# Two attention scores moved beside the attention outputs, and steps moved in the first and last groups of a two-layer graph kernel

## The chip, the cores and the metric

The kernel runs on one core of a Trainium2 chip, as one program for both layers. The metric is the device time of one execution in microseconds. Steps are called by the names that the code's own lists give them, and engines by TensorE (PE, with its weight loads PEld), VectorE (DVE), ScalarE (ACT), GpSimd (POOL) and SyncE (SP, which only issues DMAs here).

## The reference, cut to what matters

The input x is 128 graphs of 128 nodes with 512 features, adj a 128x128 matrix that all share. Everything is float32.

```python
# layer 0
h = relu(layernorm(x))
q, k, v = h @ Wq.T, h @ Wk.T, h @ Wv.T
rel = adj.T * (q @ k.T)
rel = rel / norm(rel, axis=2)
x = x + rel @ v
# layer 1: 8 heads of 64
h = relu(layernorm(x))
q, k, v = h @ Wq + bq, h @ Wk + bk, h @ Wv + bv
weights = softmax(q @ k.T / sqrt(64) + where(adj == 0, -1e9, 0))
x = x + weights @ v
```

## The kernel before, in words

**Groups and products.** Four graphs make a group (G = 4), so there are 32 groups, and a product of weights with a group's h has 512 columns. Layer 0 folds Wq and Wk into one matrix "a", so it has two products per group, G (with "a", giving gT) and V. Layer 1 has three: Q, K and V. Each product is done by a Strassen-like scheme of seven products of 256x256 quarters: class Product has steps P1 to P7, each of four matmuls of 128x128 weights and 256 columns, which show in the profile as eight MATMUL instructions of line L218. The seven use sums of weight quarters (`sums`, L88, done once) and sums of h's quarters (sumA and sumB, four additions on VectorE in each group and layer). P1, P5 and P6 are copied out of PSUM (`keep`, for layer 0, Q and K on ScalarE, for layer 1's V on VectorE), P2, P3 and P7 are added to what was kept (L242, VectorE), P4 is copied. P1, P6, P7 and P4 pile up in the same PSUM bank "x", so P4's matmuls wait for P7's addition and P6's for P1's copy; P5 and P3 share bank "z", P2 has bank "y". The pool ps_mm has four banks for all products.

**The rest of a group.** Layer 0: R (L382) is h.T with gT, mask_rel and square follow on VectorE and ScalarE, N (L408) sums the squares in four tiles of 128x32, norms turns them, O (L422) is rel times v, xO adds to x. Layer 1: S (L453) is the score of one graph for eight heads, in two row tiles of 64x128; mk adds the mask and takes the maximum (VectorE), ex takes exponentials (ScalarE, eight instructions with their sums) and sends e to DRAM, wr fetches it with its blocks turned, wt turns within blocks (VectorE). A (L570) is the output of two graphs, in two column tiles of 128x64; oc copies and sends, rdo fetches, ot turns, scales and adds to x (VectorE, then GpSimd with the store). h is turned in the same way: stat and inv (statistics, VectorE and GpSimd), hn (ScalarE, sends), rd (SP, fetches), T (VectorE). A number behind a step is its graph or pair of graphs; S0 to S3 are the four scores of a group, A0 and A1 its two outputs.

**Buffers that tie steps together.** The tiles that rd, wr and rdo fetch into (u, pool tpool) have two buffers. gT of layer 0 and v1 of layer 1 share one buffer (tag pgv). A score fills its PSUM buffer alone (ps_s has one), so S waits for the ex before it. hn, e and oT share three buffers.

**The order of work.** All five engines run in a written order: `run` (L644) walks a list of steps, and each step's instructions are queued on their engines in that order. In a cycle, l is the group in layer 1, m the next group in layer 0, n is m's layer 1 that is being prepared, f the group after it whose x is being loaded, p is l's predecessor whose outputs are being finished. FIRST (L611) is the cycle of group 0, SECOND (L618) of group 1, ORDER (L627) of groups 2 to 31, that is 30 times, LAST (L637) finishes group 31. Ahead of FIRST stand the statistics of groups 0 and 1, the DMA issues of load and load1, the folding of "a" (weights0, L117, matmuls of line L123, evicted by `place` and followed by `sums`) and the turning of layer 0's Wv (weights_v0, L133, transposes of line L139). Weights1 has layer 1's weight sums. The part of each list that TensorE does:

```python
# ORDER, TensorE's steps before the change
Q1 Q2 K1 K2 Q5 Q6 Q3 A1 Q7 K5 K6 Q4 K3 K7 G1 K4 G2 S0 G5 G6 G3 V1 G7 V2 G4 S1 V5
R V6 V3 N S2 V7 O0 O1 V4 l.V1 O2 O3 S3 l.V2 l.V5 l.V6 l.V3 l.V7 A0 l.V4
```

The last group takes S2 and S3 in halves (mkA, exA, mkB, exB), turns e on TensorE (tw), takes An for A and ends with fin, whose addition to x is on GpSimd but for the last graph, and whose store SP issues.

Of the kernel before, what the change touches and what calls it, by code (L numbers as in the profile page):

```python
# [11 lines left out]
ALU = mybir.AluOpType  # L12
# [3 lines left out]
G = 4  # L16
# [5 lines left out]
def kernel(  # L22
# [15 lines left out]
    nc = tc.nc  # L38
# [29 lines left out]
    def load(g: int, b: int, queue):  # L68
        xb = xpool.tile([P, D], F32, tag="xb", name=f"xb_{g}_{b}")
        queue.dma_start(xb, x[g * G + b])  # L70
        x_tiles[g, b] = xb
# [16 lines left out]
    def sums(n: str, w12, eng):  # L88
        c = wc[n]
        eng.tensor_tensor(c[:, T1], w12, c[:, W11], ALU.subtract)  # L90
        eng.tensor_tensor(c[:, T2], c[:, W22], c[:, T1], ALU.subtract)
        eng.tensor_tensor(c[:, T3], c[:, W22], w12, ALU.subtract)
        eng.tensor_tensor(c[:, T4N], c[:, W21], c[:, T2], ALU.subtract)
# [16 lines left out]
    w12 = {}  # L110

    def place(n: str, m: int, ps, w12, copy):

        copy(wc[n][:, W11 if m < 2 else W21, m % 2, :], ps[:, 0:HF])
        copy(w12[:, m, :] if m < 2 else wc[n][:, W22, m % 2, :], ps[:, HF:D])

    def weights0(between):  # L117

        a12 = rpool.tile([P, 2, HF], F32, tag="r", name="a12")
        pa = [ps_mm.tile([P, D], F32, tag="mm", name=f"pa_{m}") for m in range(KD)]  # L120
        for k in range(KD):
            for m in range(KD):
                nc.tensor.matmul(  # L123
                    pa[m], lhsT=raw["q"][:, k, ts(m, P)], rhs=raw["k"][:, k, :],
                    start=(k == 0), stop=(k == KD - 1),
                )
            if k == KD - 2:
                between()
        for m in range(KD):
            place("a", m, pa[m], a12, nc.vector.tensor_copy)  # L130
        sums("a", a12, nc.vector)

    def weights_v0():  # L133

        v12 = rpool.tile([P, 2, HF], F32, tag="r", name="v12")
        for m in range(KD):
            pt = ps_mm.tile([P, KD, P], F32, tag="mm", name=f"pwv_{m}")
            for k in range(KD):
                nc.tensor.transpose(pt[:, k, :], raw["v"][:, k, ts(m, P)], ident)  # L139
            place("v0", m, pt.rearrange("p k e -> p (k e)"), v12, nc.scalar.copy)  # L140
        sums("v0", v12, nc.gpsimd)
        nc.vector.tensor_scalar(mask, adj_sb, 0.0, NEG, ALU.is_equal, ALU.mult)

    def load1():
        for name, w in (("q", wq1), ("k", wk1), ("v1", wv1)):
            wr = w.rearrange("(k p) d -> p k d", p=P)
            nc.gpsimd.dma_start(
                wc[name][:, W11 : W21 + 1].rearrange("p h k d -> p (h k) d"), wr[:, :, 0:HF]
            )
            nc.gpsimd.dma_start(wc[name][:, W22], wr[:, 2:4, HF:D])  # L150
            w12[name] = wpool.tile([P, 2, HF], F32, tag="wT", name=f"w12_{name}")
            nc.gpsimd.dma_start(w12[name], wr[:, 0:2, HF:D])
        nc.gpsimd.dma_start(bq_sb, bq1.rearrange("(e p) -> p e", p=P))
        nc.gpsimd.dma_start(bk_sb, bk1.rearrange("(e p) -> p e", p=P))
        nc.gpsimd.dma_start(bv_sb, bv1.partition_broadcast(P))

    class Weights1:
        def scale(self):

            SC = HD**-0.5  # L160
            nc.scalar.mul(wc["q"][:, 0:3], wc["q"][:, 0:3], SC)
            nc.scalar.mul(w12["q"], w12["q"], SC)
            nc.scalar.mul(bq_sb, bq_sb, SC)

        def sumq(self):
            sums("q", w12["q"], nc.vector)
# [199 lines left out]
    class Layer0(Layer):  # L366
        n = 0
# [62 lines left out]
    class Layer1(Layer):  # L430
        n = 1
# [104 lines left out]
        def fin(self, b):  # L536
            g, xb = self.g, x_tiles.pop((self.g, b))
            o = work.tile([P, D], F32, tag="o", name=f"o_{g}_{b}")
            nc.vector.tensor_tensor(
                o.rearrange("p (k r d) -> p k r d", k=NH, r=2),  # L540
                self.po.pop(b).rearrange("p (k r d) -> p k r d", k=NH, r=2),
                self.rs.pop(b).rearrange("p (r k) -> p k r", r=2)[:, :, :, None].to_broadcast(
                    [P, NH, 2, HD]
                ),
                ALU.mult,
            )
            (nc.vector if b == G - 1 else nc.gpsimd).tensor_tensor(xb, xb, o, ALU.add)
            nc.sync.dma_start(out[g * G + b], xb)

        def mkA(self, b):  # L550
# [58 lines left out]


    FIRST = """  # L611
        m.sumA m.sumB m.start m.G.P1 f.hn0 f.rd0 m.G.P2 m.G.P5 w.scale m.G.P6 w.sumq m.G.P3 m.V.P1 f.hn1 f.rd1
        w.sumv m.G.P7 m.V.P2 w.sumk m.G.P4 m.V.P5
        m.R m.mask_rel m.square f.T0 m.V.P6 m.V.P3 m.N m.norms m.V.P7 m.O0 m.xO0 m.O1 m.xO1 n.stat0 n.stat1
        n.inv0 m.V.P4 n.hn0 n.rd0 f.T1 m.O2 m.O3 f.sumA f.start f.G.P1 m.xO2 m.xO3 n.stat2 n.stat3 n.inv1
        f.G.P2 f.sumB f.G.P5 n.hn1 n.rd1 f.G.P6 f.G.P3 f.G.P7 n.T0 f.G.P4 n.T1 n.start
    """.split()
    SECOND = """  # L618
        l.Q.P1 l.sumA l.Q.P2 l.sumB l.K.P1 l.K.P2 l.Q.P5 l.Q.P6 f.load0 f.load1 l.Q.P3 l.K.P5 l.K.P6 l.Q.P7
# [1 line left out]
        m.V.P2 l.S1 l.mk1 m.V.P5  # L621
        l.ex1 l.wr1 l.wt0 m.R m.mask_rel m.square f.stat2 f.stat3 f.inv1 m.V.P6 m.V.P3 m.N m.norms l.S2 l.mk2
        m.V.P7 l.ex2 l.wr2 l.wt1 m.O0 m.xO0 m.O1 m.xO1 n.stat0 n.stat1 n.inv0 m.V.P4 n.hn0 n.rd0 l.start_v l.V.P1
        m.O2 m.xO2 m.O3 m.xO3 n.stat2 n.stat3 n.inv1 l.S3 l.mk3 l.V.P2 l.V.P5 n.hn1 l.V.P6 l.wt2 n.rd1 l.ex3
        l.wr3 l.V.P3 l.V.P7 n.T0 l.A0 l.oc0 l.V.P4 n.T1 n.start
    """.split()
    ORDER = """  # L627
        l.Q.P1 p.rdo0 l.sumA l.Q.P2 m.hn0 l.sumB l.K.P1 m.rd0 m.hn1 l.K.P2 m.rd1 p.wt3 l.Q.P5
        p.ot0 l.Q.P6 l.Q.P3 p.A1 p.oc1 p.rdo1 m.T0 l.Q.P7 l.K.P5 m.T1 l.K.P6 l.Q.P4 f.load0 f.load1
        l.K.P3 m.sumA l.K.P7 m.sumB m.start m.G.P1 l.K.P4 m.G.P2 l.S0 l.mk0 m.G.P5 m.G.P6 l.ex0 l.wr0  # L630
        p.ot1 m.G.P3 m.V.P1 m.G.P7 f.stat0 f.stat1 f.inv0 m.V.P2 f.load2 f.load3 m.G.P4 l.S1 l.mk1 m.V.P5
        l.ex1 l.wr1 l.wt0 m.R m.mask_rel m.square f.stat2 f.stat3 f.inv1 m.V.P6 m.V.P3 m.N m.norms l.S2 l.mk2
        m.V.P7 l.ex2 l.wr2 l.wt1 m.O0 m.xO0 m.O1 m.xO1 n.stat0 n.stat1 n.inv0 m.V.P4 n.hn0 n.rd0 l.start_v l.V.P1
        m.O2 m.xO2 m.O3 m.xO3 n.stat2 n.stat3 n.inv1 l.S3 l.mk3 l.V.P2 l.V.P5 n.hn1 l.V.P6 l.wt2 n.rd1 l.ex3
        l.wr3 l.V.P3 l.V.P7 n.T0 l.A0 l.oc0 l.V.P4 n.T1 n.start
    """.split()
    LAST = """  # L637
        l.Q.P1 p.rdo0 l.sumA l.Q.P2 l.sumB l.K.P1 l.K.P2 p.wt3 l.Q.P5 p.ot0 l.Q.P6 l.Q.P3 l.K.P5 l.K.P6 l.K.P3
        l.Q.P7 l.S0 l.mk0 l.K.P7 l.Q.P4 l.ex0 l.wr0 l.K.P4 l.S1 l.mk1 p.A1 p.oc1 p.rdo1 l.start_v l.V.P1
        l.ex1 l.V.P2 l.V.P5 l.S2 l.mkA2 l.mkB2 l.V.P6 l.exA2 l.exB2 l.wt0 l.wr1 l.V.P3 l.V.P7 l.S3 l.mkA3 l.mkB3  # L640
        l.tw2 l.wt1 l.exA3 l.exB3 l.V.P4 l.An0 l.fin0 l.An1 l.fin1 p.ot1 l.tw3 l.An2 l.fin2 l.An3 l.fin3
    """.split()
# [1 line left out]
    def run(order, **who):  # L644
        for step in order:
            name, *path = step.split(".")
            at = who.get(name)
            if at is None:
                continue
            if len(path) == 2:  # L650
                getattr(getattr(at, path[0]), path[1])()
            elif path[0][-1].isdigit():
                getattr(at, path[0][:-1])(int(path[0][-1]))
            else:
                getattr(at, path[0])()

    with tc.manual_schedule(engines={EN.PE, EN.SP, EN.Pool, EN.DVE, EN.Activation}):
        p, l, m = None, None, Layer0(0)
        for b in range(G):
            m.stat(b)  # L660
        m.inv(0)
        m.inv(1)
        for b in range(G):
            load(1, b, nc.gpsimd)
        load1()
        m.hn_pe(0)
        m.hn_pe(1)
        f = Layer0(1)
        for b in range(G):
            f.stat(b)  # L670
        f.inv(0)
        f.inv(1)
        weights0(lambda: m.turn_pe(0))
        m.turn_pe(1)
        weights_v0()
        for g in range(NG):
            n = Layer1(g)
            if g:
                f = Layer0(g + 1) if g + 1 < NG else None
            run((FIRST, SECOND, ORDER)[min(g, 2)], p=p, l=l, m=m, n=n, f=f, w=Weights1())  # L680
            p, l, m = l, n, f
        run(LAST, p=p, l=l)
# [30 lines left out]
```

## Time and profile before

| what | us |
|---|---|
| median of three runs | 2524.23 (2522.88 to 2525.54) |
| the profiled execution | 2526.15 |
| its span, first to last instruction | 2524.4 |
| TensorE busy (matmuls) | 2497.9 |
| VectorE, ScalarE, GpSimd busy | 1709.2, 1022.3, 534.7 |
| a steady cycle (from one l.Q.P1 to the next) | 77.14 |
| first matmul, last matmul's end | 4.29, 2514.8 |

TensorE's matmuls overlap: one is listed with the time from its start to its end, while the next starts before that end. So durations of matmuls are read from start to start. The mean granted clock of TensorE is 0.997 of full speed.

### The profile page before, as it was taken

The numbers are of one execution on the slowest core, as the hardware profiler recorded it, in microseconds if no ns is written. First come the engines' busy times: TensorE is split into PE (matmuls) and PEld (weight loads), VectorE is DVE, ScalarE is ACT, GpSimd is POOL, SyncE is SP. The second block draws the span as 40 slices with busy tenths as digits, with TensorE's granted clock in tenths as the row PEclk, the third lists the DMA queues.
The fourth block names the chain that finished last, engine by engine and source line by source line (L and its number), as shares of the span: only waits on it lengthen the run. The fifth ranks groups of instructions, "written<-read, shape, count | busy, mean of one in ns | idle before, by whom it ended". The sixth has DMA issues, their size and how long they took to land.

```text
span 2524.4 us, 40790 instructions
## 1 busy us (share of the span) xinstructions
PE 2497.9 (99%) x14672; PEld 2106.7 (83%) x14672; DVE 1709.2 (68%) x2484; ACT 1022.3 (40%) x3248; POOL 534.7 (21%) x945
## 2 busy tenths in 40 slices
PE   8999999999999999999999999999999999999998
PEld 6788888888888888888888888888888888888886
DVE  5566766676776667666767766676667676666766
ACT  3344443444433444344444434443444444344433
POOL 4121222112122212221121222122211212221211
PEclk9999999999999999999999999999999999999999
DMA  5255554556445555445564455554455644555543
GB/s 172 84 176 175 166 156 141 182 161 199 147 145 159 176 175 167 152 147 176 160 197 146 144 165 173 178 167 152 147 175 162 197 148 143 164 176 176 167 135 101
DMA packets 370475, 405.71 MB, mean 161 GB/s; under 512 B 29600, under 2 KB 286752, under 8 KB 370272
## 3 DMA queue, kind: packets, MB, share of 16 engines
q1 hardware_dynamic: 278992, 167.92, 25.2%
q10 hardware_dynamic: 70384, 166.74, 18.4%
q0 software_dynamic: 20896, 68.44, 8.2%
q8 instruction: 115, 1.88, 0.3%
q14 instruction: 88, 0.72, 0.1%
HBM read 204.80 MB, written 198.18 MB: 160 GB/s over the span
## 4 chain that ended last, share of the span: by engine, by line
PE 97%; DVE 1%; DMA 1%; ACT 0%; issue 0%; POOL 0%; SPq 0%; ACTq 0%; DVEq 0%; POOLq 0%
PE pv_x L218 18%; PE pq_x L218 9%; PE pv_z L218 9%; PE pk_x L218 9%; PE pg_x L218 9%; PE pss L453 6%; PE po L570 5%; PE pv_y L218 5%; PE pg_z L218 4%; PE pq_z L218 4%; PE pr L382 4%; PE pk_z L218 4%; PE po L422 4%; PE pk_y L218 2%; PE pg_y L218 2%; PE pq_y L218 2%
## 5 line engine op out<-in xcount | busy, mean ns | idle before, releaser
L471 ACT ACTIVATE e<-pss,nmax 128x128 f32<-128x128 f32 x1008 | 354.1, 379 | 178.0 <-DVE nmax L464 156.2
L605 POOL TENSOR_TENSOR xb<-xb,o 128x512 f32<-128x512 f32 x124 | 158.3, 1276 | 1108.8 <-DVE o L598 1083.9
L218 PE MATMUL pv_x<-wc_v,h 128*128 128x256 f32 x1280 | 300.8, 382 | 0.0
L218 PEld LDWEIGHTS pv_x<-wc_v,h 128*128 128x128 f32 x1280 | 240.3, 190 | 51.0 <-DVE v L242 11.8
L301 ACT ACTIVATE hn<-xb,shift,rstd 128x512 f32<-128x512 f32 x252 | 190.9, 807 | 153.5 <-POOL shift L293 153.4
L313 DVE STREAM_TRANSPOSE h<-u_h 128x1024 f32<-128x1024 f32 x126 | 156.4, 1242 | 133.0 <-DMA u_h<-d_h 130.4
L218 PE MATMUL pv_z<-wc_v,s 128*128 128x256 f32 x1024 | 246.0, 383 | 0.0
L471 ACT ACTIVATION_READ_ACCUMULATOR e<-pss,nmax 128x1 f32 x1008 | 220.7, 219 | 0.0
L218 PEld LDWEIGHTS pv_z<-wc_v,s 128*128 128x128 f32 x1024 | 192.6, 191 | 29.2 <-DVE pv_r L235 0.4
L462 DVE TENSOR_TENSOR pss<-pss,mask 128x1024 f32<-128x1024 f32 x126 | 154.7, 1228 | 81.0 <-PE pss L453 75.5
L218 PE MATMUL pv_x<-wc_v,s 128*128 128x256 f32 x768 | 184.9, 384 | 0.0
L218 PE MATMUL pq_x<-h,wc_q 128*128 128x256 f32 x768 | 184.8, 383 | 0.0
L283 DVE BATCH_NORM_STATS2 st<-xb 128x6 f32<-128x512 f32 x256 | 172.1, 672 | 16.0 <-DMA xb<-in_x_dram 16.0
L218 PE MATMUL pk_x<-h,wc_k 128*128 128x256 f32 x768 | 181.5, 379 | 0.0
L453 PEld LDWEIGHTS pss<-kT,qT 64*128 64x128 f32 x2048 | 124.2, 187 | 54.4 <-issue 27.0
L218 PEld LDWEIGHTS pq_x<-h,wc_q 128*128 128x128 f32 x768 | 143.2, 190 | 23.8 <-ACT oT L581 5.1
L218 PEld LDWEIGHTS pk_x<-h,wc_k 128*128 128x128 f32 x768 | 145.8, 190 | 19.9
L290 POOL TENSOR_SCALAR rstd<-mv 128x2 f32<-128x2 f32 x128 | 28.9, 226 | 630.0 <-DVE mv L284 629.8
L218 PEld LDWEIGHTS pv_x<-wc_v,s 128*128 128x128 f32 x768 | 140.8, 190 | 20.5 <-issue 0.2
L464 DVE TENSOR_REDUCE nmax<-pss 128x8 f32<-128x1024 f32 x126 | 154.3, 1224 | 4.3
L486 DVE STREAM_TRANSPOSE wT<-u_w 128x1024 f32<-128x1024 f32 x126 | 150.7, 1196 | 5.2 <-DMA u_w<-d_w 5.0
L453 PE MATMUL pss<-kT,qT 64*128 64x128 f32 x2048 | 148.7, 285 | 2.6 <-ACT e L471 2.3
(147 smaller groups left out, 4416.8 us busy)
## 6 DMA issues: line engine op xcount, KB each, us to landing
d_h<-hn ACTq DMA_DIRECT2D x126, 512.0 KB, 3.6
u_h<-d_h SPq DMA_DIRECT2D x504, 128.0 KB, 3.5
d_w<-e ACTq DMA_DIRECT2D x126, 512.0 KB, 2.7
u_w<-d_w SPq DMA_DIRECT2D x504, 128.0 KB, 3.1
xb<-in_x_dram POOLq DMA_DIRECT2D x124, 256.0 KB, 3.3
d_o<-oT ACTq DMA_DIRECT2D x62, 512.0 KB, 4.3
u_o<-d_o SPq DMA_DIRECT2D x248, 128.0 KB, 3.6
out_dram<-xb POOLq DMA_DIRECT2D x124, 256.0 KB, 3.0
```

What stands on the lines that cost most here:

```text
L218: nc.tensor.matmul(ps[:, m, :], lhsT=lhsT, rhs=rhs, start=first and m == 0 and k == 0, stop=k == 1, skip_group_check=True,)
L283: nc.vector.bn_stats(st, x_tiles[g, b])
L301: nc.scalar.activation(hn[:, r], x_tiles[g, b].rearrange("p (k j q) -> p j k q", j=TB, q=BK), AF.Relu, bias=self.shift[:, b : b + 1], scal ...
L313: nc.vector.transpose(half.rearrange("p k (t i) -> p t k i", i=BK), self.u.pop(i).rearrange("p t (k q) -> p t k q", q=BK),)
L382: nc.tensor.matmul(pr[:, b, :], lhsT=self.turned(k, b), rhs=self.gT[:, k, ts(b, P)], start=(k == 0), stop=(k == KD - 1),)
L453: nc.tensor.matmul(pss[:, r, k, :], lhsT=self.qT[rows, k, ts(b, P)], rhs=self.kT[rows, k, ts(b, P)], start=True, stop=True,)
L462: nc.vector.tensor_tensor(sc, sc, mask[:, None, :].to_broadcast([P, H, P]), ALU.add)
L464: nc.vector.tensor_reduce(self.nmax[b], sc, AX.X, ALU.max, negate=True)
L471: nc.scalar.activation(e[:, :, i, :], sc[:, i, :].rearrange("p (j q) -> p j q", q=BK), AF.Exp, bias=nmax[:, i : i + 1], accum_out=self.tot ...
L486: nc.vector.transpose(self.wT[b].rearrange("p h (t i) -> p t h i", i=BK), self.uw.pop(b).rearrange("p t (h q) -> p t h q", q=BK),)
L570: nc.tensor.matmul(po[r * HD : (r + 1) * HD, k, :], lhsT=self.v[:, b, ts(2 * k + r, HD)], rhs=wT[:, r * NH + k, :], start=True, stop=True,)
L605: nc.gpsimd.tensor_tensor(xb, xb, o.rearrange("p k t q -> p (k t q)"), ALU.add)
```

## The change

In ORDER, S3 (with mk3 and ex3) moves from behind O3 to just ahead of A0, and A1 (with oc1 and rdo1) moves from behind Q3 to just behind S0. The fetch wr3 goes over into the next cycle, behind p.rdo0, and p.wt3 moves from ahead of l.Q.P5 to behind l.Q.P7. p.ot0 now stands ahead of l.Q.P5 and l.Q.P6, m.hn1 and m.rd1 stand behind l.Q.P6, m.T1 behind l.K.P3, p.ot1 behind m.G.P7; f.stat2, f.stat3 and f.inv1 move behind n.hn1, f.load2 and f.load3 behind l.wr1. TensorE's steps in ORDER after the change:

```python
Q1 Q2 K1 K2 Q5 Q6 Q3 Q7 K5 K6 Q4 K3 K7 G1 K4 G2 S0 A1 G5 G6 G3 V1 G7 V2 G4 S1 V5
R V6 V3 N S2 V7 O0 O1 V4 l.V1 O2 O3 l.V2 l.V5 l.V6 l.V3 l.V7 S3 A0 l.V4
```

SECOND's end is changed in the same way (S3 with A0). In FIRST the statistics of group 1, until now ahead of weights0, are taken behind m.sumB; the sums of layer 0's Wv (sumw, GpSimd) follow behind f.inv1; sumq moves behind m.V.P2, sumk behind f.sumB, xO2 and xO3 ahead of f.sumA; group 2's x is loaded (loadx) behind w.sumv and no longer in SECOND. In LAST ex0 goes ahead of l.Q.P4, wr3 and wt3 get places, and fin's addition for graph 2 is on VectorE too.

```diff
-        sums("v0", v12, nc.gpsimd)
+        w12["v0"] = v12
...
+        def sumw(self):
+            sums("v0", w12["v0"], nc.gpsimd)
+
+        def loadx(self):
+            for b in range(G):
+                load(2, b, nc.gpsimd)
...
-            (nc.vector if b == G - 1 else nc.gpsimd).tensor_tensor(xb, xb, o, ALU.add)
+            (nc.vector if b >= G - 2 else nc.gpsimd).tensor_tensor(xb, xb, o, ALU.add)
...
     FIRST = """
-        m.sumA m.sumB m.start m.G.P1 f.hn0 f.rd0 m.G.P2 m.G.P5 w.scale m.G.P6 w.sumq m.G.P3 m.V.P1 f.hn1 f.rd1
-        w.sumv m.G.P7 m.V.P2 w.sumk m.G.P4 m.V.P5
+        m.sumA m.sumB m.start f.stat0 f.stat1 f.inv0 m.G.P1 m.G.P2 f.stat2 f.stat3 f.inv1 w.sumw m.G.P5 f.hn0 f.rd0 m.G.P6
+        w.scale m.G.P3 m.V.P1 f.hn1 f.rd1 w.sumv w.loadx m.G.P7 m.V.P2 w.sumq m.G.P4 m.V.P5
...
-        n.inv0 m.V.P4 n.hn0 n.rd0 f.T1 m.O2 m.O3 f.sumA f.start f.G.P1 m.xO2 m.xO3 n.stat2 n.stat3 n.inv1
-        f.G.P2 f.sumB f.G.P5 n.hn1 n.rd1 f.G.P6 f.G.P3 f.G.P7 n.T0 f.G.P4 n.T1 n.start
+        n.inv0 m.V.P4 n.hn0 n.rd0 f.T1 m.O2 m.xO2 m.O3 m.xO3 n.stat2 n.stat3 n.inv1 f.sumA f.start f.G.P1
+        f.G.P2 f.sumB w.sumk f.G.P5 n.hn1 n.rd1 f.G.P6 f.G.P3 f.G.P7 n.T0 f.G.P4 n.T1 n.start
...
     ORDER = """
-        l.Q.P1 p.rdo0 l.sumA l.Q.P2 m.hn0 l.sumB l.K.P1 m.rd0 m.hn1 l.K.P2 m.rd1 p.wt3 l.Q.P5
-        p.ot0 l.Q.P6 l.Q.P3 p.A1 p.oc1 p.rdo1 m.T0 l.Q.P7 l.K.P5 m.T1 l.K.P6 l.Q.P4 f.load0 f.load1
-        l.K.P3 m.sumA l.K.P7 m.sumB m.start m.G.P1 l.K.P4 m.G.P2 l.S0 l.mk0 m.G.P5 m.G.P6 l.ex0 l.wr0
-        p.ot1 m.G.P3 m.V.P1 m.G.P7 f.stat0 f.stat1 f.inv0 m.V.P2 f.load2 f.load3 m.G.P4 l.S1 l.mk1 m.V.P5
-        l.ex1 l.wr1 l.wt0 m.R m.mask_rel m.square f.stat2 f.stat3 f.inv1 m.V.P6 m.V.P3 m.N m.norms l.S2 l.mk2
+        l.Q.P1 p.rdo0 l.sumA l.Q.P2 p.wr3 m.hn0 l.sumB l.K.P1 m.rd0 l.K.P2 p.ot0 l.Q.P5 l.Q.P6 m.hn1 m.rd1
+        l.Q.P3 l.Q.P7 p.wt3 m.T0 l.K.P5 l.K.P6 l.Q.P4 f.load0 f.load1 l.K.P3 m.T1
+        l.K.P7 m.sumA m.sumB m.start m.G.P1 l.K.P4 m.G.P2 l.S0 p.A1 l.mk0 p.oc1 p.rdo1 m.G.P5 m.G.P6
+        l.ex0 l.wr0 m.G.P3 m.V.P1 m.G.P7 p.ot1 m.V.P2 f.stat0 f.stat1 f.inv0 m.G.P4 l.S1 l.mk1 m.V.P5
+        l.ex1 l.wt0 l.wr1 f.load2 f.load3 m.R m.mask_rel m.square m.V.P6 m.V.P3 m.N m.norms l.S2 l.mk2
...
-        m.O2 m.xO2 m.O3 m.xO3 n.stat2 n.stat3 n.inv1 l.S3 l.mk3 l.V.P2 l.V.P5 n.hn1 l.V.P6 l.wt2 n.rd1 l.ex3
-        l.wr3 l.V.P3 l.V.P7 n.T0 l.A0 l.oc0 l.V.P4 n.T1 n.start
+        m.O2 m.xO2 m.O3 m.xO3 n.stat2 n.stat3 n.inv1 l.V.P2 l.V.P5 n.hn1 f.stat2 f.stat3 f.inv1 l.V.P6 l.wt2
+        n.rd1 l.V.P3 l.V.P7 n.T0 l.S3 l.A0 l.mk3 l.oc0 l.V.P4 l.ex3 n.T1 n.start
     LAST = """
-        l.Q.P1 p.rdo0 l.sumA l.Q.P2 l.sumB l.K.P1 l.K.P2 p.wt3 l.Q.P5 p.ot0 l.Q.P6 l.Q.P3 l.K.P5 l.K.P6 l.K.P3
-        l.Q.P7 l.S0 l.mk0 l.K.P7 l.Q.P4 l.ex0 l.wr0 l.K.P4 l.S1 l.mk1 p.A1 p.oc1 p.rdo1 l.start_v l.V.P1
+        l.Q.P1 p.rdo0 l.sumA l.Q.P2 p.wr3 l.sumB l.K.P1 l.K.P2 p.ot0 l.Q.P5 l.Q.P6 l.Q.P3 p.wt3 l.K.P5 l.K.P6 l.K.P3
+        l.Q.P7 l.S0 l.mk0 l.K.P7 l.ex0 l.wr0 l.Q.P4 l.K.P4 l.S1 l.mk1 p.A1 p.oc1 p.rdo1 l.start_v l.V.P1
...
-        for b in range(G):
-            f.stat(b)
-        f.inv(0)
-        f.inv(1)
```

More of the change, by code (lines that the diff above doesn't have):

```diff
@@ L623 @@
         m.V.P7 l.ex2 l.wr2 l.wt1 m.O0 m.xO0 m.O1 m.xO1 n.stat0 n.stat1 n.inv0 m.V.P4 n.hn0 n.rd0 l.start_v l.V.P1
-        m.O2 m.xO2 m.O3 m.xO3 n.stat2 n.stat3 n.inv1 l.S3 l.mk3 l.V.P2 l.V.P5 n.hn1 l.V.P6 l.wt2 n.rd1 l.ex3
-        l.wr3 l.V.P3 l.V.P7 n.T0 l.A0 l.oc0 l.V.P4 n.T1 n.start
+        m.O2 m.xO2 m.O3 m.xO3 n.stat2 n.stat3 n.inv1 l.V.P2 l.V.P5 n.hn1 l.V.P6 l.wt2
+        n.rd1 l.V.P3 l.V.P7 n.T0 l.S3 l.A0 l.mk3 l.oc0 l.V.P4 l.ex3 n.T1 n.start
     """.split()
     ORDER = """
-        l.Q.P1 p.rdo0 l.sumA l.Q.P2 m.hn0 l.sumB l.K.P1 m.rd0 m.hn1 l.K.P2 m.rd1 p.wt3 l.Q.P5
@@ L633 @@
+        l.Q.P3 l.Q.P7 p.wt3 m.T0 l.K.P5 l.K.P6 l.Q.P4 f.load0 f.load1 l.K.P3 m.T1
+        l.K.P7 m.sumA m.sumB m.start m.G.P1 l.K.P4 m.G.P2 l.S0 p.A1 l.mk0 p.oc1 p.rdo1 m.G.P5 m.G.P6
+        l.ex0 l.wr0 m.G.P3 m.V.P1 m.G.P7 p.ot1 m.V.P2 f.stat0 f.stat1 f.inv0 m.G.P4 l.S1 l.mk1 m.V.P5
+        l.ex1 l.wt0 l.wr1 f.load2 f.load3 m.R m.mask_rel m.square m.V.P6 m.V.P3 m.N m.norms l.S2 l.mk2
         m.V.P7 l.ex2 l.wr2 l.wt1 m.O0 m.xO0 m.O1 m.xO1 n.stat0 n.stat1 n.inv0 m.V.P4 n.hn0 n.rd0 l.start_v l.V.P1
-        m.O2 m.xO2 m.O3 m.xO3 n.stat2 n.stat3 n.inv1 l.S3 l.mk3 l.V.P2 l.V.P5 n.hn1 l.V.P6 l.wt2 n.rd1 l.ex3
@@ L635 @@
-        l.wr3 l.V.P3 l.V.P7 n.T0 l.A0 l.oc0 l.V.P4 n.T1 n.start
+        m.O2 m.xO2 m.O3 m.xO3 n.stat2 n.stat3 n.inv1 l.V.P2 l.V.P5 n.hn1 f.stat2 f.stat3 f.inv1 l.V.P6 l.wt2
+        n.rd1 l.V.P3 l.V.P7 n.T0 l.S3 l.A0 l.mk3 l.oc0 l.V.P4 l.ex3 n.T1 n.start
     """.split()
     LAST = """
-        l.Q.P1 p.rdo0 l.sumA l.Q.P2 l.sumB l.K.P1 l.K.P2 p.wt3 l.Q.P5 p.ot0 l.Q.P6 l.Q.P3 l.K.P5 l.K.P6 l.K.P3
-        l.Q.P7 l.S0 l.mk0 l.K.P7 l.Q.P4 l.ex0 l.wr0 l.K.P4 l.S1 l.mk1 p.A1 p.oc1 p.rdo1 l.start_v l.V.P1
+        l.Q.P1 p.rdo0 l.sumA l.Q.P2 p.wr3 l.sumB l.K.P1 l.K.P2 p.ot0 l.Q.P5 l.Q.P6 l.Q.P3 p.wt3 l.K.P5 l.K.P6 l.K.P3
```

## The prediction

> **What bounds the kernel now.** I read the page's busy line and chain first, then a table of busy time by stage, then TensorE's timeline. From the page:
>
> ```profile
> PE 2497.9 (99%) x14672; PEld 2106.7 (83%) x14672; DVE 1709.2 (68%) x2484; ACT 1022.3 (40%) x3248; POOL 534.7 (21%) x945
> PE 97%; DVE 1%; DMA 1%; ACT 0%; issue 0%; POOL 0%; SPq 0%; ACTq 0%; DVEq 0%; POOLq 0%
> ```
>
> The table by stage (length; busy PE, PEld, DVE, ACT, POOL; clock) says where TensorE is idle:
>
> ```profile
> 0.00:77.83 77.83, 66.95 (x280) 49.70 (x281) 43.14 (x73) 23.86 (x40) 37.03 (x59) 0.96 0.53 173
> 77.83:144.38 66.55, 63.37 (x369) 52.92 (x368) 37.65 (x57) 25.84 (x92) 6.41 (x17) 1.00 0.31 95
> 144.38:2458.98 2314.60, 2314.60 (x13682) 1958.10 (x13681) 1589.61 (x2302) 951.02 (x3030) 480.01 (x858) 1.00 0.53 164
> 2458.98:2524.40 65.42, 52.95 (x345) 45.94 (x343) 38.79 (x52) 21.61 (x86) 11.22 (x11) 0.94 0.34 108
> ```
>
> In the 30 steady cycles TensorE has no idle time at all: 2314.60 of 2314.60 us, 77.14 us each. A steady cycle gets shorter only if TensorE's own work does. Idle time lies in the first 90 us and the last 40. The timeline (start, length, line, out<-in, count) shows what in TensorE's work is not streaming:
>
> ```profile
> 1203.78 1.88 PE L422 MATMUL po<-v,rel 128*128 128x512 f32 x4
> 1205.49 3.62 PE L218 MATMUL pv_x<-wc_v,h 128*128 128x256 f32 x16
> 1208.95 1.88 PE L422 MATMUL po<-v,rel 128*128 128x512 f32 x4
> 1210.76 1.16 PE L453 MATMUL pss<-kT,qT 64*128 64x128 f32 x16
> 1211.85 1.99 PE L218 MATMUL pv_y<-wc_v,h 128*128 128x256 f32 x8
> 1213.68 1.89 PE L218 MATMUL pv_z<-wc_v,s 128*128 128x256 f32 x8
> ...
> 1218.86 1.89 PE L218 MATMUL pv_x<-wc_v,h 128*128 128x256 f32 x8
> 1220.68 1.97 PE L570 MATMUL po<-wT,v 128*64 128x128 f32 x32
> 1222.58 1.99 PE L218 MATMUL pv_x<-wc_v,h 128*128 128x256 f32 x8
> 1224.41 1.89 PE L218 MATMUL pq_x<-h,wc_q 128*128 128x256 f32 x8
> ```
>
> Read start to start. A product step takes 1.73 us (3.46 for two from 1205.49), O takes 1.71. O before S takes 1.81, the product after S 1.83: a score S among 128*128 work costs 1.09 + 0.10 + 0.10 = 1.29. An output A costs 0.09 before it, 1.90, and 0.10 after: 2.09. The last group has the two side by side already:
>
> ```profile
> 2486.59 1.16 PE L453 MATMUL pss<-kT,qT 64*128 64x128 f32 x16 [1.99 <-ACT e L471]
> 2487.69 1.97 PE L570 MATMUL po<-wT,v 128*64 128x128 f32 x32
> 2489.58 1.99 PE L218 MATMUL pv_x<-wc_v,h 128*128 128x256 f32 x8
> 2491.41 1.89 PE L218 MATMUL pv_y<-wc_v,h 128*128 128x256 f32 x8
> ```
>
> S to A is 1.10, A to product 1.89, and one surcharge of 0.10 follows. With an entry of 0.09 ahead of S that is 3.18 for the pair, against 1.29 + 2.09 = 3.38 apart: 0.20 less. Three stalls of the start:
>
> ```profile
> 24.63 3.48 PE L139 MATMUL pwv<-ident,raw_v 128*128 128x128 f32 x16 [3.10 <-issue]
> 43.96 2.92 PE L218 MATMUL pg_x<-h,wc_a 128*128 128x256 f32 x8 [2.03 <-DVE gT L242]
> 87.47 1.99 PE L218 MATMUL pq_z<-s,wc_q 128*128 128x256 f32 x8 [2.57 <-DVE qT L242]
> ```
>
> **What the Trainium skill says.** "TensorEngine Tiling (Array Packing)", section "Key Properties": a change of tiling mode, not of the tile alone, drains TensorE. The trace agrees, with about 0.2 us for each change; it is the count of changes that the edit lowers. "TensorE: Matmul & The Clock Gate", section "What's actually happening": after an idle window TensorE is clocked at half rate. Here matmuls that follow one another at 0.216 us go at 0.427 for 3.4 us behind the stall at 43.96. "DMA: Bandwidth & Descriptors", section "Issuing engines are not separate DMA queues": DMAs of all queues share the 16 engines and interleave. The trace agrees: the last part of one fetch of hn landed 5.65 us after its issue while an e tile was being sent (2.9 us otherwise).
>
> **1. S beside A.** In an ORDER cycle S0 goes with A1 and S3 with A0; in SECOND S3 with A0. That is 30 x 2 + 1 = 61 pairs at 0.20 us: 12.2 us, all on the path. Bounds: 0 if a pair keeps both drains; 12.2 as the pair of the last group shows it.
>
> **2. What the order has to bear for that.** I laid the new lists against a cycle of 76.75 us (t = 0 at l.Q.P1), TensorE's steps at the durations above, and followed each moved step. Durations: product on TensorE to its reader 1.93, DVE add 0.6 to 0.7, mask and maximum of a score 2.45, ex 2.93 and 0.37 to issue its send, hn 1.5 and 0.37, send to landing 2.8 to 3.7, four fetches 1.4 to issue and 2.9 more for the last to land (2.5 to 5.7 occur).
> - *S3, mk3, ex3, wr3 late.* l.S3 is at 71.9, but mk3 now stands behind n.T0 on DVE, whose fetch lands at about 74.3 (ex3's send, which slowed it, is gone from that place). n.T0 to 75.6, mk3 to 78.0, which is t = 1.3 of the next cycle; ex3 and its send hold ACT to 4.7, and the first copy of l.Q.P1 (ready at 1.93) waits behind it, to 5.5; its add on DVE to 6.2. l.Q.P5 needs that PSUM bank at 6.9: 0.7 to spare, no cost. m.hn0 follows on ACT; its fetch (p.rdo0 and p.wr3 are ahead of it on SP) lands by 15, m.T0 is due at 22.5.
> - *p.ot0 ahead of m.T0 and m.T1, p.wt3 later.* A fetch needs one of two u buffers, so m.rd1 waits for p.wt3 (DVE, to 16.0) and for m.hn1's send (about 16.4); its four parts are issued to 18 and land at 21.5, with 0.65 added for a load of x that crosses it. m.T1 runs 21.6 to 22.9, then the add of l.K.P7 to 23.5; l.K.P4 needs it at 24.2: 0.6 to spare.
> - *A1 late.* gT and v1 share one buffer, so DVE's add of m.G.P2 waits for p.A1 (end 30.9), and mk0 behind it ends at 34. ex0 ends by 38; S1, which needs its bank, is due at 43. p.oc1, p.rdo1 and p.ot1 follow: p.ot1 (3.3 us) starts on DVE at 40.3, V.P2's add and two statistics behind it, so mk1 starts at 45.8 instead of 44.2. ex1 ends with its send at 51.6, square at 52.2, and N on TensorE is due at 53.0: 0.8 to spare. The fetch for l.wt1 lands 1 us later and moves DVE's steps from m.xO0 to l.V.P6's bias addition by as much; l.V.P7 on TensorE is due 0.3 after that addition.
> - *f.stat2, f.stat3, f.inv1, f.load2, f.load3.* 1.6 us of DVE and 2 us of POOL move to where DVE has the 2.45 us that mk3 left. The loads wait for p.ot1's stores; they are used 15 us later. No cost.
>
> So every dependence fits, by 0.3 to 0.8 us, and I take no stall. If the cover is gone, each 0.1 us of stall costs 3 us over 30 cycles.
>
> **3. The start.** DVE waits for the x of group 1 until 19.44 and evicts pa only from 23.80, behind four statistics. These move behind m.sumB. The last pa are done from 18.1 to 20.65, so DVE evicts them at once and ends the a sums at 23.9 (26.43 + 2.6 = 29.0 before). The 3.10 us of idle ahead of pwv go, and its 16 transposes, 0.218 us each, run at the 0.109 of the pt transposes: m.G.P1 starts at 23.2 instead of 27.95, 4.7 us. w.sumq (DVE 35.85 to 42.6, slowed from 0.7 to 1.7 an operation beside POOL) no longer stands ahead of G.P3's and G.P7's adds: 2.03 of idle and eight matmuls at half clock (8 x 0.21 = 1.7) go, 3.7 us. It now stands ahead of mask_rel, which is ready at 44.6; sumq ends near 45, and sq is needed at 47.9: no cost. w.sumw and the f.inv steps stay where POOL is free, from 28.4 when its DMA issues end. n.T1 waited 7.02 us for a fetch that shared the engines with four loads of x (POOL 70.61 to 72.9); w.loadx puts them near 45, w.sumk moves under f.G.P3, and m.xO2 and m.xO3 no longer stand behind f.sumA: n.T1 at about 72, needed at 76: 2.6 us. The stalls of 0.68 (O2) and 0.79 (f.G.P4) stay. Sum 11.0; between 6 (one new stall of 3 us with its half clock) and 12. I take 10, since f.hn0 now delays the copy that m.G.P7 needs, and other small waits will show.
>
> **4. The end.** ex0 goes ahead of l.Q.P4's copy on ACT, so it starts at 2481.8 instead of 2483.6 and S1's stall of 1.99 shrinks to 0.1: 1.9 us. fin2's addition moves from POOL to DVE (0.7 to 1.3 us), but fin3's addition, 1.95 us beside POOL's, falls to about 0.7, and it no longer ends last by that much: 1.1 us. Sum 3.0; between 1.9 and 3.5.
>
> **Sum.** The profiled execution took 2526.15 us (span 2524.4 and 1.75 around it). 12.2 + 10 + 3 = 25.2, so 2501.0; the median of the runs is 1.9 below that execution: **2499**.
>
> **Rivals.**
> - *The small margins are not there.* ACT's late copy of l.Q.P1, square before N, l.V.P6's addition: one of them stalls each cycle by 0.1 to 0.8 us. For it: four margins below 1 us, from rows that vary by some tenths. Against: durations repeat to 0.01 us in the trace. 2499 + 30 x 0.1 to 0.8 = 2502 to 2523, most likely about 2508.
> - *Slower: l.K.P4 waits for m.T1.* In ORDER the add of l.K.P7 is queued behind m.T1 on DVE. If m.rd1's last part lands at 23.6 and not 21.5 (4.8 us from issue were seen for fetches that crossed loads and stores, and p.ot0's stores and f.load0, f.load1 now fall there), TensorE stalls 1.4 us in each cycle: 42 us, 2541. It decides from 25.2 / 30 = 0.84 us of stall a cycle.
> - *The pair saves nothing* because S to A drains like two changes: start and end remain, 2524 - 13 = 2511. Against it stands the last group's pair.
>
> **Chances.** Forecast 0.62 (2495 to 2503), small margins 0.20, l.K.P4 0.11, no saving 0.07. The range reaches to 2514, which takes in no saving and most of the small margins. About 0.2% (5 us) is what a measurement can tell from no change. Faster: 0.62 + 0.17 + 0.02 + 0.07 = 0.88; within: 0.03 + 0.02 = 0.05; slower 0.07.
>
> **What would show it.** In the changed profile: pss L453 followed by po L570 after 1.10 us, twice a cycle; cycles of 76.75 us with no idle TensorE; pwv without its 3.10, the stalls at 43.96 and 87.47 gone, m.G.P1 near 23. Wrong: a wait of TensorE on DVE kT or qT L242, on ACT sq, or a cycle of 77 us and more.

## The result, and the profile after

The changed kernel takes 2554.14 us (2553.69 to 2554.62, four runs) against 2524.22 us: 1.0119 times as long, 95% interval 1.0104 to 1.0134. It was to be 1% faster and is 1.2% slower. Its profiled execution has a span of 2552.4 us. The page's busy line and chain:

```profile
PE 2501.7 (98%) x14672; PEld 2108.9 (83%) x14672; DVE 1704.2 (67%) x2485; ACT 1020.2 (40%) x3248; POOL 532.5 (21%) x944
PE 65%; DMA 14%; DVE 11%; ACT 4%; issue 3%; SPq 3%; POOL 0%; ACTq 0%; DVEq 0%
```

The chain no longer lies on TensorE alone: transfers and VectorE have a quarter of it. The table by stage of the changed kernel (length, then busy PE, PEld, DVE, ACT, POOL), cut at the first l.Q.P1, the second, and the last:

```profile
0.00:70.08 70.08, 63.90 (x280) 47.21 (x281) 42.49 (x73) 23.39 (x40) 35.65 (x59) 1.00 0.61 199
70.08:133.19 63.11, 62.83 (x369) 52.93 (x368) 35.79 (x56) 22.98 (x76) 6.41 (x17) 1.00 0.27 86
133.19:2490.14 2356.95, 2322.02 (x13682) 1962.87 (x13682) 1586.54 (x2304) 949.25 (x3030) 480.53 (x858) 1.00 0.51 161
2490.14:2552.40 62.26, 52.95 (x345) 45.94 (x343) 39.40 (x54) 24.56 (x102) 9.94 (x10) 0.96 0.37 118
```

Against the four lengths of before (77.83, 66.55, 2314.60, 65.42) that is -7.75, -3.44, +42.35 and -3.16 us, together +28.0, the whole difference of the two spans (2552.4 - 2524.4). Start and end together brought about what was forecast. The 30 steady cycles, which had no idle TensorE, now have 34.9 us of it, and last 78.57 us on average.

Which wait it is, TensorE's own list of waits says (who waited, for whom: us in total, times, longest):

```profile
PE pk_x L225 <- DVE kT L249: 30.5, 25, 2.7
PE pa L123 <- DMA raw_q<-in_L_gnn_Wq_dram: 4.4, 1, 4.4
PE pv_x L225 <- DVE pv_r L242: 1.1, 6, 0.2
PE pq_x L225 <- DVE h L320: 1.0, 3, 0.5
PE po L429 <- DVE xb L435: 0.9, 2, 0.7
```

L225 and L249 are the lines L218 and L242 of before. A matmul into K's bank x waits for an addition into kT: that is l.K.P4, which waits for the addition of l.K.P7. One of the longest waits, first on TensorE's timeline, then on VectorE's:

```profile
1567.40 1.89 PE L225 MATMUL pg_x<-h,wc_a 128*128 128x256 f32 x8
1572.01 3.50 PE L225 MATMUL pk_x<-h,wc_k 128*128 128x256 f32 x8 [2.72 <-DVE kT L249]
1575.35 1.89 PE L225 MATMUL pg_y<-h,wc_a 128*128 128x256 f32 x8
```

```profile
1565.94 0.69 DVE L249 TENSOR_TENSOR kT<-pk_z,pk_r 128x512 f32<-128x512 f32 x1 [0.78 <-PE pk_z L225]
1570.14 1.25 DVE L320 STREAM_TRANSPOSE h<-u_h 128x1024 f32<-128x1024 f32 x1 [3.50 <-DMA u_h<-d_h]
1571.31 0.65 DVE L249 TENSOR_TENSOR kT<-pk_x,pk_r 128x512 f32<-128x512 f32 x1
```

VectorE has done l.K.P3's addition by 1566.63 and stands still for 3.50 us, since the next instruction in its queue is m.T1, whose fetch has not landed. The addition of l.K.P7, whose product is done, is queued behind. TensorE starts l.K.P4 at 1572.01, and then at half clock: its eight matmuls take 3.34 us from start to start instead of 1.83. The prediction named this as the rival "Slower: l.K.P4 waits for m.T1".

In the kernel before, m.T1 waited for its fetch too, but ahead of l.K.P3's addition:

```profile
1244.14 1.25 DVE L313 STREAM_TRANSPOSE h<-u_h 128x1024 f32<-128x1024 f32 x1 [2.25 <-DMA u_h<-d_h]
1247.49 0.69 DVE L242 TENSOR_TENSOR kT<-pk_z,pk_r 128x512 f32<-128x512 f32 x1 [2.11 <-PE pk_z L218]
```

On average over the 30 cycles this wait was 2.26 us before and is 1.74 us now. So VectorE does not wait longer for m.T1; what is new is which addition stands behind it.

The pair itself is there. A cycle of the changed kernel on TensorE's timeline:

```profile
1416.55 1.16 PE L460 MATMUL pss<-kT,qT 64*128 64x128 f32 x16
1417.64 1.97 PE L577 MATMUL po<-wT,v 128*64 128x128 f32 x32
1419.54 1.99 PE L225 MATMUL pg_z<-s,wc_a 128*128 128x256 f32 x8
```

S to A is 1.09, A to the product 1.90, and the two cycles in which nothing waited last 76.75 us each, 0.39 less than 77.14.

Where the 30 cycles lose time, place by place: for each instruction of TensorE, the time from the start of the one before it, less the smallest such time among the 30 cycles, so half clock behind a stall counts too.

| place | us over 30 cycles, changed kernel | before |
|---|---|---|
| l.K.P4 | 43.6 | 0.2 |
| l.V.P7 | 3.5 | 0.2 |
| l.Q.P5 | 3.4 | 0.2 |
| next l.Q.P1 | 1.9 | 0.1 |
| O2 | 1.8 | 0.1 |

These five are 54.2 us. Less the 30 x 0.39 = 11.7 us that the pairs save, that is 42.5, against the 42.35 us by which the 30 cycles are longer. And 54.2 on top of the forecast's 2499 is 2553.2, against 2554.14 measured: the lost time is in these places. Of l.K.P4's 43.6 us, 30.5 are the waits of the list above and 6.3 are half clock, behind four of the 25 waits; the rest lies around the stops, since the list counts a wait only from the end that it gives to the matmul before.

### The profile page after: what moved, and what is told of

The parts are those of the page before. It is cut to its first block, busy times and chain, and to the rows that moved or that the text cites. A ratio compares the mean times of both kernels' runs of the same rounds, so it can differ in the third digit from the quotient of the medians.

```text
span 2552.4 us, 40841 instructions
## 1 busy us (share of the span) xinstructions
PE 2501.7 (98%) x14672; PEld 2108.9 (83%) x14672; DVE 1704.2 (67%) x2485; ACT 1020.2 (40%) x3248; POOL 532.5 (21%) x944
## 3 DMA queue, kind: packets, MB, share of 16 engines
q10 hardware_dynamic: 70384, 166.74, 17.3%
## 4 chain that ended last, share of the span: by engine, by line
PE 65%; DMA 14%; DVE 11%; ACT 4%; issue 3%; SPq 3%; POOL 0%; ACTq 0%; DVEq 0%
PE pv_x L225 12%; DMA u_h<-d_h 8%; PE pg_x L225 7%; PE pv_z L225 6%; PE pk_x L225 5%; PE pss L460 4%; PE pg_z L225 4%; PE pq_x L225 4%; PE pr L389 4%; PE po L577 4%; DMA d_h<-hn 4%; PE pv_y L225 3%; PE po L429 3%; SPq L199 3%; PE pq_z L225 3%
## 5 line engine op out<-in xcount | busy, mean ns | idle before, releaser
L225 PE MATMUL pv_x<-wc_v,h 128*128 128x256 f32 x1280 | 301.6, 382 | 1.2 <-DVE pv_r L242 1.1
L225 PEld LDWEIGHTS pv_x<-wc_v,h 128*128 128x128 f32 x1280 | 239.6, 190 | 55.0 <-DVE v L249 11.7
L225 PE MATMUL pv_z<-wc_v,s 128*128 128x256 f32 x1024 | 245.1, 382 | 0.0
L225 PE MATMUL pk_x<-h,wc_k 128*128 128x256 f32 x768 | 190.6, 392 | 30.5 <-DVE kT L249 30.5
L225 PEld LDWEIGHTS pv_z<-wc_v,s 128*128 128x128 f32 x1024 | 191.6, 190 | 29.0
L225 PEld LDWEIGHTS pk_x<-h,wc_k 128*128 128x128 f32 x768 | 147.7, 195 | 61.2 <-DVE kT L249 41.1
L225 PE MATMUL pv_x<-wc_v,s 128*128 128x256 f32 x768 | 184.9, 384 | 0.0
L225 PE MATMUL pq_x<-h,wc_q 128*128 128x256 f32 x768 | 182.0, 380 | 1.2 <-DVE h L320 1.0
L588 ACT COPY oT<-po 128x512 f32<-128x512 f32 x124 | 72.7, 586 | 252.4 <-PE po L577 252.4
L225 PEld LDWEIGHTS pq_x<-h,wc_q 128*128 128x128 f32 x768 | 145.3, 190 | 22.7 <-PE pv_x L225 2.7
L225 PEld LDWEIGHTS pv_x<-wc_v,s 128*128 128x128 f32 x768 | 140.8, 190 | 20.6 <-issue 0.2
```

The costliest lines, as they stand in the source:

```text
L225: nc.tensor.matmul(ps[:, m, :], lhsT=lhsT, rhs=rhs, start=first and m == 0 and k == 0, stop=k == 1, skip_group_check=True,)
```

## The experiments

Theory after the result: l.K.P4 waits because the addition of l.K.P7 stands behind m.T1 on VectorE, and m.T1's fetch is late because m.hn1's send and m.rd1's fetch cross other transfers, that is, run while these run. Rivals: a late fetch costs the same wherever the addition stands; the lateness comes from SP's queue and not from crossing; the pair's gain comes from other moves.

**The addition ahead of the transpose.**

```diff
-        l.Q.P3 l.Q.P7 p.wt3 m.T0 l.K.P5 l.K.P6 l.Q.P4 f.load0 f.load1 l.K.P3 m.T1
-        l.K.P7 m.sumA
+        l.Q.P3 l.Q.P7 p.wt3 m.T0 l.K.P5 l.K.P6 l.Q.P4 f.load0 f.load1 l.K.P3
+        l.K.P7 m.T1 m.sumA
```

> The changed kernel with one swap in ORDER: l.K.P7 ahead of m.T1, so that VectorE's addition of l.K.P7 no longer stands behind the transpose that waits for m.rd1. Theory (the addition is queued behind a late fetch): TensorE's wait of l.K.P4 goes, 43.6 us over 30 cycles; m.T1 still starts near 23.4 us of the cycle, and the sums that m.G.P5 needs are ready by 26 against 30.7. The other small waits stay (10.9 us over 30 cycles): cycles of 77.1 on average, 2510 us. Rival (the fetch is late, and whoever needs it waits, wherever the addition stands): the wait turns up at m.G.P5 or at l.K.P4 all the same, and the time stays above 2540.

Measured: 2508.33 us, 0.9932 of before (0.9918 to 0.9947). TensorE's list has no wait on kT any more; behind two waits of the start, the next in it are

```profile
PE pq_x L225 <- DVE h L320: 0.8, 3, 0.4
PE po L429 <- ACT v L233: 0.7, 1, 0.7
PE po L429 <- DVE xb L435: 0.6, 2, 0.4
PE pv_x L225 <- DVE pv_r L242: 0.5, 3, 0.2
```

and VectorE's timeline shows the new order, l.K.P7's addition and then the same wait for the fetch, which now delays only the sums of h:

```profile
1382.89 0.69 DVE L249 TENSOR_TENSOR kT<-pk_z,pk_r 128x512 f32<-128x512 f32 x1 [3.83 <-PE pk_z L225]
1384.55 0.69 DVE L249 TENSOR_TENSOR kT<-pk_x,pk_r 128x512 f32<-128x512 f32 x1 [0.97 <-PE pk_x L225]
1385.75 1.25 DVE L320 STREAM_TRANSPOSE h<-u_h 128x1024 f32<-128x1024 f32 x1 [0.50 <-DMA u_h<-d_h]
1387.03 0.69 DVE L363 TENSOR_TENSOR s<-h 128x512 f32<-128x512 f32 x1
```

The fetch is as late as in the changed kernel (last part at 23.38 us of the cycle on average, 23.43 there). So its lateness alone costs nothing at l.K.P4 (0.2 us over 30 cycles); what cost 46 us is what was queued behind it. One swap of two names in a list is the difference between 1.2% slower and 0.7% faster.

**Start and end alone.** The changed kernel with SECOND and ORDER of before.

> The changed kernel's prologue, FIRST, LAST and fin with SECOND and ORDER of before (LAST without p.wr3). Theory (start and end brought what was forecast, the loss is in ORDER): 30 cycles of 77.14, first l.Q.P1 at 70.1 instead of 77.8, some 3 us less in SECOND, 3 less at the end: 2510.5 us. Rival (the new start delays later cycles too, through x tiles and weight sums): above 2520.

Measured: 2512.61 us, 0.9950 (0.9935 to 0.9965). The first l.Q.P1 is at 69.31, SECOND takes 63.30, the last group 62.30, the 30 cycles 2315.06: start, SECOND and end are 14.9 us shorter than before, and the 30 cycles are 0.5 longer, so the new start delays next to nothing later.

**Loads of x out of the way of m.rd1.**

```diff
-                load(self.g, b, nc.gpsimd)
+                load(self.g, b, nc.sync if b < 2 and self.g > 2 else nc.gpsimd)
...
-        l.K.P6 l.Q.P4 f.load0 f.load1 l.K.P3 m.T1
+        l.K.P6 l.Q.P4 l.K.P3 m.T1
...
-        l.S0 p.A1 l.mk0 p.oc1 p.rdo1 m.G.P5
+        l.S0 p.A1 l.mk0 p.oc1 p.rdo1 f.load0 f.load1 m.G.P5
```

> The changed kernel with f.load0 and f.load1 of ORDER issued by SP behind p.rdo1 instead of by GpSimd behind p.ot0's stores, so that no load of x crosses m.rd1's fetch. Theory (m.rd1 lands at 23.4 instead of 21.5 because it and m.hn1's send cross p.ot0's stores and these loads): the last part of m.rd1 lands about 0.7 us sooner in the cycle, TensorE's wait at l.K.P4 falls from 1.45 to about 0.8 us a cycle: 2534 us. Rival (the lateness is m.rd1's place in SP's queue and the u buffers, not the crossing): landing and time as in the changed kernel, 2554 us.

Measured: 2514.81 us, 0.9960 (0.9945 to 0.9975). The direction was right, the size was twice what was expected: m.rd1's last part lands 1.4 us sooner, and the wait at l.K.P4 falls to 7.3 us over 30 cycles.

```profile
PE pk_x L225 <- DVE kT L249: 4.8, 7, 1.0
```

**Without p.ot0's stores.**

```diff
-                nc.gpsimd.dma_start(out[g * G + b], xb)
+                if i or g == NG - 1:
+                    nc.gpsimd.dma_start(out[g * G + b], xb)
```

> The changed kernel without the two stores of p.ot0 (graphs 0 and 1 of every group but the last are not written to the output); everything else is as it was, and the loads of x that waited for these stores may start sooner. Theory (the crossing of p.ot0's stores with m.hn1's send makes that send 1 us longer): m.hn1's send lands at 16.4 instead of 17.4 us of the cycle, the last part of m.rd1 at 22.0 or sooner, TensorE's wait at l.K.P4 falls to 0.3 us a cycle or less: about 2519 us. Rival (not the crossing): m.hn1's send lands at 17.4 still, 2554 us.

This kernel leaves out two of the four stores of every group but the last. Measured: 2514.58 us, 0.9956 (0.9940 to 0.9973). The wait at l.K.P4 falls to 6.4 us over 30 cycles, but not in the way expected: the send lands only 0.36 us sooner, at 17.04. The loads, free of the stores they waited for, start at 13.9 and 14.6 us of the cycle instead of 16.2 and 18.6 and have landed at 18.4 and 19.2, ahead of most of m.rd1's fetch. So this run shows the loads' crossing once more. It does not price the stores' crossing: the two loads, of the same size as the stores, now run beside the send in their place. Means over the 30 cycles, in us from l.Q.P1, from the start and landing times of the trace:

| | m.hn1's send issued | landed | m.rd1's last part issued | landed | addition of l.K.P7 ends |
|---|---|---|---|---|---|
| forecast | not given | 16.4 | 18.0 | 21.5 | 23.5 |
| changed | 12.96 | 17.40 | 18.89 | 23.43 | 25.37 |
| loads late | 12.92 | 17.46 | 18.99 | 22.04 | 24.08 |
| no stores | 12.92 | 17.04 | 18.61 | 22.00 | 23.99 |

**A1 beside S0 alone, in the kernel before.**

```diff
-        l.Q.P3 p.A1 p.oc1 p.rdo1 m.T0
+        l.Q.P3 m.T0
...
-        l.S0 l.mk0 m.G.P5 m.G.P6 l.ex0 l.wr0
-        p.ot1 m.G.P3 m.V.P1 m.G.P7 f.stat0
+        l.S0 p.A1 l.mk0 p.oc1 p.rdo1 m.G.P5 m.G.P6 l.ex0 l.wr0
+        m.G.P3 m.V.P1 m.G.P7 p.ot1 f.stat0
```

> The kernel before with one part of the change in ORDER alone: p.A1, p.oc1 and p.rdo1 moved behind S0 and p.ot1 behind m.G.P7; S3, all other steps, start and end as before. Theory (one drain less per pair, and the late A1 costs nothing, since m.hn1, m.rd1 and m.T1 keep their early places): 30 x 0.20 = 6 us less, cycles of 76.95: 2519 us. Rival (A1's lateness delays mk1, square and N through gT's buffer and p.ot1): cycles of 77.2 and more, 2526 us or above.

Measured: 2537.99 us, 1.0050 (1.0037 to 1.0063): slower, as the rival had it, but only in part by the rival's path. TensorE's waits on VectorE in that kernel that were not there before:

```profile
PE pv_z L218 <- DVE pv_r L235: 3.6, 9, 0.8
...
PE pv_x L218 <- DVE v L242: 1.2, 1, 1.2
PE pq_x L218 <- DVE qT L242: 1.1, 2, 0.7
PE po L422 <- DVE v L242: 1.1, 1, 1.1
```

By place, l.V.P3 (which waits for l.V.P5's addition; in this order mk3 is still ahead of it on VectorE) loses 9.4 us over 30 cycles, l.Q.P4 6.0. The 30 cycles take 2326.8 us, 12.2 more than before.

The 9.4 us are the rival's path, further along than it said: on average mk1 starts at 45.92 us of the cycle (44.40 before), l.wt1 at 58.86 (57.98) and mk3 at 66.44 (65.90), while N loses nothing. The 6.0 us have another cause. With A1 gone from behind Q3, TensorE comes to l.Q.P4 at 17.39 us of the cycle instead of 19.37, but the addition of l.Q.P7, which stands behind p.ot0 and m.T0 on VectorE, ends at 17.18 (17.29 before). In the changed kernel, where p.ot0 and p.wt3 have moved too, it ends at 14.84 and l.Q.P4 loses 0.2 us. So A1's move leans on other moves of the change; no run takes these one at a time, so which of them it needs is not shown.

**Both pairs taken apart by one product**, in the version with l.K.P7 ahead of m.T1.

```diff
-        l.S0 p.A1 l.mk0 p.oc1 p.rdo1 m.G.P5 m.G.P6
+        l.S0 l.mk0 m.G.P5 p.A1 p.oc1 p.rdo1 m.G.P6
...
-        n.rd1 l.V.P3 l.V.P7 n.T0 l.S3 l.A0 l.mk3
+        n.rd1 l.V.P3 l.S3 l.V.P7 n.T0 l.A0 l.mk3
```

> The version with l.K.P7 ahead of m.T1 (2508.3 us), with both pairs of ORDER taken apart by one product: m.G.P5 between S0 and A1, l.V.P7 between S3 and A0; VectorE's order is kept but for nothing. Theory (a pair saves one change of tiling mode, 0.20 us): 2 x 30 x 0.20 = 12 us more, 2520 us, cycles from 76.75 to 77.14 where nothing waits. Rival (the gain came from the other moves, the pair saves nothing): 2508 us.

Measured: 2516.52 us, 0.9966 (0.9953 to 0.9978), 8.2 more than the pairs. Cycles without a wait last 77.14 instead of 76.75: 0.39 for two pairs, as forecast. The 30 cycles take 9.6 us more (2319.5 against 2309.9) and not 12, mainly since l.V.P7, now behind S3, no longer waits for l.V.P6's addition (2.5 us over 30 cycles in the version with the pairs); N loses 1.0 in return.

**l.wt1 behind the statistics**, on top of the swap.

```diff
-        m.V.P7 l.ex2 l.wr2 l.wt1 m.O0 m.xO0 m.O1 m.xO1 n.stat0 n.stat1 n.inv0 m.V.P4
+        m.V.P7 l.ex2 l.wr2 m.O0 m.xO0 m.O1 m.xO1 n.stat0 n.stat1 n.inv0 l.wt1 m.V.P4
```

> The version with l.K.P7 ahead of m.T1, and l.wt1 in ORDER moved behind n.inv0, so that xO0, xO1 and the statistics do not stand behind the transpose that waits for its fetch. Theory (the small waits left, of l.Q.P5, O2, l.V.P7 and the next l.Q.P1, come from that fetch by way of n.hn0, n.T0 and mk3): these waits, 7.6 us over 30 cycles, mostly go: 2502 us. Rival (they come from ex3 and the additions ahead of them, whatever wt1 does): 2508 us.

Measured: 2500.19 us, 0.9901 (0.9888 to 0.9915), the best version with the next one. Of its table by stage, the row of the 30 cycles:

```profile
133.22:2436.19 2302.97, 2302.90 (x13682) 1963.43 (x13682) 1597.13 (x2304) 949.36 (x3030) 480.79 (x858) 1.00 0.52 165
```

TensorE is idle for 0.07 us in 2303, and 28 of the 30 cycles last 76.75. With this the forecast's 2499 is reached, by an order in which its assumption of no stall holds.

**f.stat2 and f.stat3 ahead of n.T0**, on top of that.

```diff
-        m.O2 m.xO2 m.O3 m.xO3 n.stat2 n.stat3 n.inv1 l.V.P2 l.V.P5 n.hn1 f.stat2 f.stat3 f.inv1 l.V.P6 l.wt2
-        n.rd1 l.V.P3 l.V.P7 n.T0
+        m.O2 m.xO2 m.O3 m.xO3 n.stat2 n.stat3 n.inv1 l.V.P2 l.V.P5 n.hn1 l.V.P6 l.wt2
+        n.rd1 l.V.P3 l.V.P7 f.stat2 f.stat3 f.inv1 n.T0
```

> As the version with l.wt1 moved, and f.stat2, f.stat3 and f.inv1 moved from behind n.hn1 to behind l.V.P7, ahead of n.T0, where VectorE waits for a fetch. Theory: l.V.P7 no longer waits for l.V.P6's addition in any cycle, and n.T0 is not later than before since its fetch lands after these statistics: 2501 us. Rival (the statistics now delay n.T0, mk3 and ex3): l.Q.P5 or the next l.Q.P1 waits, 2506 us or more.

Measured: 2500.12 us, 0.9899 (0.9884 to 0.9914), the same as without: moving l.wt1 had already freed l.V.P7. It tells no more than that.

## Why the prediction was wrong

- **The pair: right.** 0.39 us for two pairs, in the waitless cycles of the changed kernel (76.75) and in the pairs taken apart (77.14). From S to A it is 1.09 us, as from S to a full product, and A takes 1.90 from its start to the next product, as it does alone: S to A costs one change of mode, not two, as the pair of the last group had shown. What is saved is, by the Trainium skill ("TensorEngine Tiling (Array Packing)", section "Key Properties"), a drain of TensorE at a change of tiling mode; the page gives no price, the trace gives 0.2 us.
- **Start: right in sum.** Forecast 11.0 by its steps and 10 taken. The first l.Q.P1 comes 7.75 us earlier (4.7 + 3.7 = 8.4 forecast) and SECOND is 3.44 shorter, of which 0.20 is its pair (3.24, where 2.6 was forecast): 11.0. That the sum is exact is luck, since two errors of 0.65 cancel. m.G.P1 starts at 23.72 (forecast 23.2), l.Q.P5 without its 2.57, and G.P4 without its 2.03 and the half clock.
- **End: right.** 3.0 forecast, 3.1 measured.
- **No stall in a cycle: wrong, and here is the step.** The forecast said that m.rd1's parts "land at 21.5", that the addition of l.K.P7 ends at 23.5, "0.6 to spare". The parts land at 23.43 and the addition ends at 25.37 on average. The path was right: the fetch starts 0.12 us behind the landing of m.hn1's send, with p.wt3 done at 16.06 (16.0 forecast). Two terms of it were too small. The send, issued at 12.96, was to land at "about 16.4", which leaves it 3.4 us; it took 4.44. The last part of the fetch was to take 2.9 + 0.65 = 3.5 us from issue to landing; it took 4.54. Together 1.9 us, which turns 0.6 to spare into a stall of 1.3; the measured loss is 1.45 a cycle, of which 0.2 is half clock.
- **What made the two terms larger.** I had charged the fetch with one crossing load of 0.65; with both loads away it takes 3.05, so the two cost 1.5. I had charged the send with no crossing at all, though it has p.ot0's stores and m.rd0's fetch beside it. That fetch was itself late: the forecast had it land "by 15", and its last part lands at 17.25 on average. In the version with l.wt1 later it lands at 15.77, and the same send takes 3.72. So its crossing is a likely cause, but there the stores came 0.8 us sooner too, and no run changed the fetch or the stores alone: how the send's extra 1.0 us divides between them is left open.
- **The margins of 0.3 to 0.8.** l.Q.P5 and l.V.P7, with 0.7 and 0.3 to spare on paper, lost 3.4 and 3.5 us over 30 cycles; l.Q.P1, behind n.T0, 1.9, and O2 1.8, were not among my margins. N with its 0.8 lost nothing. The cause was l.wt1 ahead of xO0, as its move shows: these four places lose 7.6 us over 30 cycles in the version with the swap, and 0.9 after it. The move takes away both l.wt1's wait for its fetch (0.97 us a cycle) and its 1.3 us of work from ahead of xO0; the runs do not part the two.
- **The chances.** The rival at 0.11 had the place, the mechanism, the landing (23.6; measured 23.43) and the price (42 us; measured 43.6, though 6.3 of these are half clock, which the rival did not count). Its 2541 was short of 2554 mainly by the small waits (10.6 us), which it left out. What spoke for it, a margin of 0.6 us against a fetch whose last part lands anywhere from 21.8 to 25.4 us of the cycle, deserved more: in the kernel before, the same part already landed anywhere from 17.3 to 21.4. A margin smaller than the spread of the transfer in front of it is no margin: a late transfer stalls TensorE, while an early one gives nothing back.

## What to carry to other kernels

In an engine's in-order queue, the instruction that waits for a transfer decides when everything behind it runs; put the additions that the bounding engine needs ahead of it, and let the late transfer delay only what is needed late. When steps are moved, lay out what else is on the DMA engines at the new time, each transfer there as a price of its own. And a change of TensorE's tiling mode costs about 0.2 us, so small tiled products belong next to one another, as long as the engines behind them bear it.

## What the runs showed of the hardware that was not expected

- The Trainium skill ("TensorE: Matmul & The Clock Gate", section "What's actually happening") speaks of an idle window of some 3.4 us ahead of the half clock. Here shorter stalls were enough: behind stalls of 2.18, 2.27, 2.60 and 2.72 us at l.K.P4 the trace records half clock, each time for 3.41 us. Behind stalls of 1.64, 1.79 and 2.52 us at the same place it records none, nor behind the 2.57 us at 87.47 in the kernel before. So the length of a stall alone did not decide it.
- Two loads of 256 KB that cross a fetch of four parts of 128 KB lengthen its last part from 3.05 to 4.54 us from issue to landing (loads late against the changed kernel, means over 30 cycles).
